# Layer 0 softmax sums in 32-column blocks beside the heads' sums, reciprocals spread by transfers, in a fused graph-attention and multi-head-attention kernel

## Chip, cores and metric

The kernel runs on one core of one Trainium2 chip. The metric is the device time of one execution in microseconds, the median over several runs. Before the change it is 2849.53 us (three runs, 2846.7 to 2849.74).

## What is computed

The input x has 64 groups of 256 tokens of width 512, and adj is a 256 x 256 mask of edges, the same for all groups. Two layers follow each other; everything is in 32-bit floats.

```python
# layer 0: graph attention, added to x
h = maximum(layernorm(x), 0)
Wh = h @ W
logits = (Wh @ a_src)[:, :, None] + (Wh @ a_dst)[:, None, :]
logits = where(logits >= 0, logits, 0.2 * logits)      # then -inf where adj == 0
x = x + softmax(logits, axis=-1) @ Wh

# layer 1: attention with 8 heads of width 64, added to x
h = maximum(layernorm(x), 0)
q, k, v = heads(h @ Wq.T + bq), heads(h @ Wk.T + bk), heads(h @ Wv.T + bv)
scores = q @ k^T / 8                                   # then -inf where adj == 0
x = x + merge(softmax(scores, axis=-1) @ v) @ Wo.T + bo
```

Both softmaxes are computed without a maximum taken off: exponentials are multiplied by a 0/1 mask, summed, and the sums' reciprocals are multiplied in. It is the sums and reciprocals of layer 0 that the change touches.

## The kernel before

One group (256 tokens, two tiles of 128 partitions) passes through a chain of stages, each a Python generator that yields between parts of its work. A hand-written list, `first_half + second_half`, is walked once for each group i; an entry such as `(aggregate0, 2)` runs the next part of that stage for group i + 2. The list is therefore the program order of every engine: each engine works through its own instructions in that order and waits by semaphores for the others. SyncE (SP) issues nearly all transfers, in the same order. PSUM has 8 banks, handed out in turn by `bank`.

The stages that matter here, with the engine that does the work:

- `weights0` (lines 518 to 561, entry E0, two groups ahead): ScalarE makes the exponentials, VectorE their maximum (L537), GpSimd applies the mask (`em`, L540) and adds the two halves of the source nodes into `esum`, 128 partitions x 256 columns (L542). In its third part TensorE multiplies `esum` by a 128 x 128 matrix of ones (L556): the product holds the softmax sum of each of the 256 target nodes in every one of 128 partitions. VectorE takes the maximum with 1e-38 (L558) and the reciprocal (L559), over 256 columns, into a tile of tag `rb0`.
- `quarters0` (L566 to 593, entry Q0, two ahead): GpSimd combines quarters of h, multiplies `em` by the reciprocals (L578) and makes four differences `eq` (L588). These are the operands of a seven-product (Strassen-like) multiplication, used for groups from PLAIN = 3 on. Groups 0 to 2 take a plain one.
- `aggregate0` (L595 to 648, entry U0, then US): seven products of h and the scaled edge weights (L606), four and then three, with sums on VectorE; ScalarE copies the first.
- `normalize0` and `normalize1` (entries N0 and N1): statistics on ScalarE, closed by three short GpSimd operations (L474 to L476), then the normalization on ScalarE; `transpose1` (X1) transposes the result of normalize1 on TensorE (L750).
- `attention` (L825 to 924, entries A and A_OLD): scores (L838), exponentials, masks (L851) and sums over the two halves (L853); then `values` (L863) and `head_sums` (L873). There eight matmuls put the sums of the 8 heads into one bank: the stationary operand `half` is 32 columns wide, so pair e of heads fills partitions 32e to 32e + 31. VectorE takes the reciprocal (L886), and eight transfers (L909), issued by SyncE, spread one row each, 256 columns, over 64 partitions of the tile `rb`. `scale` (entry AS) multiplies `aT` by it on VectorE (L936), and `output` (entry O) uses `aT` in products with Wo (L207).

For a group g, `head_sums` runs in the iteration g + 1, at the A_OLD with which the second half begins. The third E0 of that iteration, at the end of the first half, belongs to group g + 3.

Of the kernel before, what the change touches and what calls it, by code (L numbers as in the profile page):

```python
# [9 lines left out]
F32 = mybir.dt.float32  # L10
# [6 lines left out]
P = 128  # L17
# [6 lines left out]
Q = 32  # L24
# [4 lines left out]
def kernel(  # L29
# [26 lines left out]
    nc = tc.nc  # L56
    B, N, D = x.shape
    NC = N // P
    DC = D // P
    NT = GB * NC  # L60
    TOK = NT * P
    G = B // GB
    DH = D // HEADS
# [18 lines left out]
    ones = const.tile([P, P], F32, tag="ones", name="ones")  # L82
# [49 lines left out]
    def bounded():  # L132
        weights = ctx_b.enter_context(tc.tile_pool(name="weights", bufs=1))
        big = ctx_b.enter_context(tc.tile_pool(name="big", bufs=1))
        work = ctx_b.enter_context(tc.tile_pool(name="work", bufs=1))
# [3 lines left out]
        def bank(shape, name):  # L139
            return ps_mm.tile(shape, F32, tag="mm", name=name)  # L140
# [207 lines left out]
        pick = weights.tile([P, P], F32, tag="pick", name="pick")  # L348
# [10 lines left out]
        def constants():  # L359

            ok = weights.tile([P, 2 * DC + 5], F32, tag="ok", name="ok")
            rows = weights.tile([P, 2 * DC], F32, tag="rows", name="rows")
            gms = []
            for n in range(2):
                w_q = whole((wq_sb, wk_sb)[n])  # L370

                gm = work.tile([P, DC, DH], F32, tag="gram", name=f"gram_{n}", bufs=2)
                gms.append(gm)
                for pair in range(2):
                    pg = bank([P, 2, DH], f"pgram_{n}_{pair}")
                    for e in range(2):
                        for c in range(DC):
                            for r in range(2):
                                at = e * P + r * DH
                                wc = w_q[c // 2][pair][:, c % 2, at : at + DH]  # L380
                                nc.tensor.matmul(
                                    pg[r * DH : (r + 1) * DH, e, :], wc, wc,
                                    start=(c == 0), stop=(c == DC - 1),
                                )
                    yield
                    nc.vector.tensor_copy(gm[:, 2 * pair : 2 * pair + 2, :], pg)
                    yield
            for n, gm in enumerate(gms):
                pgs = [bank([P, DC, DH], f"pgram2_{n}_{r}") for r in range(2)]
                for e in range(DC):  # L390
                    for r in range(2):
                        half_p = slice(r * DH, (r + 1) * DH)
                        part = gm[half_p, e, :]
                        nc.tensor.matmul(pgs[r][half_p, e, :], part, part, start=True, stop=True)
                yield
                for e in range(DC):
                    for r in range(2):
                        half_p = slice(r * DH, (r + 1) * DH)
                        ab = work.tile([P, DH], F32, tag="gabs", name=f"gabs_{n}_{e}_{r}")
                        nc.scalar.activation(  # L400
                            ab[half_p], pgs[r][half_p, e, :], AF.Abs,
                            accum_out=rows[half_p, n * DC + e : n * DC + e + 1],
                        )
                yield
            for _ in range(10):
                yield
            sq = weights.tile([P, 4], F32, tag="sq", name="sq")
            for j, col in enumerate((cols["bq"], cols["bk"])):
                junk = work.tile([P, DC], F32, tag="e2", name=f"junk_c_{j}")
                nc.vector.scalar_tensor_tensor(  # L410
                    junk, col, 1.0, col, op0=ALU.mult, op1=ALU.mult, accum_out=sq[:, j : j + 1]
                )
            for _ in range(4):
                yield
            pq = bank([P, 2], "pq")
            nc.tensor.matmul(pq, ones, sq[:, 0:2], start=True, stop=True)
            yield
            nc.vector.tensor_scalar(
                ok[:, 2 * DC + 2 : 2 * DC + 4], pq, 1.0, None, op0=ALU.is_le
            )  # L420
            yield
            for j in range(2):
                junk = work.tile([P, D], F32, tag="e2", name=f"junk_w_{j}")
                nc.vector.scalar_tensor_tensor(
                    junk, wa[j], 1.0, wa[j], op0=ALU.mult, op1=ALU.mult, accum_out=sq[:, 2 + j : 3 + j]
                )
                yield
            nc.vector.tensor_scalar(ok[:, 0 : 2 * DC], rows, 1.0, None, op0=ALU.is_le)
            nc.vector.tensor_scalar(ok[:, 2 * DC : 2 * DC + 2], sq[:, 2:4], 1.95, None, op0=ALU.is_le)
            yield  # L430
            big_v = weights.tile([P, 1], F32, tag="big_v", name="big_v")
            nc.vector.tensor_reduce(big_v, svs, AX.X, ALU.add)
            nc.vector.tensor_scalar(
                ok[:, 2 * DC + 4 : 2 * DC + 5], big_v, 1.0e6, None, op0=ALU.is_le
            )
            okm = weights.tile([P, 1], F32, tag="okm", name="okm")
            nc.vector.tensor_reduce(okm, ok, AX.X, ALU.min)
            for _ in range(12):
                yield
            pk = bank([1, 1], "pok")  # L440
            nc.tensor.matmul(pk, okm, ones[:, 0:1], start=True, stop=True)
            nc.vector.tensor_scalar(flag, pk, P - 0.5, None, op0=ALU.is_lt)
            yield
            picks()
            yield

        class Stats:

# [30 lines left out]
        nodes, edges, sums0, lefts, norms, qkv, vs, outs = {}, {}, {}, {}, {}, {}, {}, {}  # L479
# [38 lines left out]
        def weights0(g):  # L518
# [22 lines left out]
            esum = work.tile([P, N], F32, tag="esum", name=f"esum_{g}")  # L541
            engine.tensor_tensor(esum, em[:, 0, :], em[:, 1, :], op=ALU.add)  # L542
            edges[g] = [em]
            yield

            if g == 0:
                ps = bank([P, NT], f"ps_{g}")
                for t in range(NT):
                    nc.tensor.matmul(
                        ps[:, t : t + 1], esum[:, t * P : (t + 1) * P], ones[:, 0:1],  # L550
                        start=True, stop=True,
# [7 lines left out]
            nc.vector.reciprocal(rs, rs)  # L559
            edges[g].append(rs)  # L560
            yield


        PLAIN = 3

        def quarters0(g):  # L566

# [257 lines left out]
        def attention(g):  # L825
# [30 lines left out]
            def values(j, pair):  # L856
# [13 lines left out]
                aT.append(work.tile([P, 2, N], F32, tag=f"aT{j}", name=f"aT{j}_{g}"))  # L870
                nc.scalar.copy(aT[j], pav)  # L871

            def head_sums():  # L873

                psm = bank([P, N], f"psm_{g}")
                for r in range(2):
                    for e in range(DC):
                        nc.tensor.matmul(
                            psm[e * Q : (e + 1) * Q, :],
                            half[:, r, :],  # L880
                            sums[e][:, r, :],
                            start=(r == 0),
                            stop=(r == 1),
                        )
                rc = work.tile([P, N], F32, tag="rc", name=f"rc_{g}")
                nc.vector.reciprocal(rc, psm)  # L886
                return rc

            exs = [scores(e) for e in range(DC)]
# [4 lines left out]
            if g == G - 1:  # L894
# [3 lines left out]
                rc = head_sums()  # L898
                values(1, exs[2:4])
            else:  # L900
                for j in range(2):
                    values(j, exs[2 * j : 2 * j + 2])
                rc = head_sums()
            if g < G - 2:
                rb = work.tile([P, DC, N], F32, tag="rb", name=f"rb_{g}")
                for e in range(DC):
                    for r in range(2):
                        src = rc[e * Q + r * (Q // 2) : e * Q + r * (Q // 2) + 1, :]
                        nc.sync.dma_start(  # L909
                            rb[r * DH : (r + 1) * DH, e, :],  # L910
                            bass.AP(
                                tensor=src.tensor, offset=src.offset,
                                ap=[src.ap[0], [0, DH], [1, N]],
                            ),
                        )
            else:

                yield
                rb = [bank([P, N], f"prb_{g}_{e}") for e in range(DC)]
                for e in range(DC):  # L920
                    rows = slice(e * Q, (e + 1) * Q)
                    nc.tensor.matmul(rb[e], pick[rows, :], rc[rows, :], start=True, stop=True)
            outs[g] = aT, rb
            yield

# [89 lines left out]
        def aside(n=1):  # L1015
            for _ in range(n):
                next(side, END)

        K, V, W, O = (project_qk, 0), (project_v, 0), (transform0, 1), (output, -2)
        N0, D0, E0, U0 = (normalize0, 3), (normalize0, 2), (weights0, 2), (aggregate0, 2)  # L1020
        Q0 = (quarters0, 2)
        US, N1, X1 = (aggregate0, 1), (normalize1, 1), (transpose1, 1)
        A, A_OLD, BO = (attention, 0), (attention, -1), (bias_rows, 0)
        AS, AS_OLD = (scale, -1), (scale, -2)
        first_half = [
            (load, 3), O, D0, K, AS_OLD, O, K, O, K, E0, O, K, E0, O, US, A_OLD, K, O, K, BO, O, K, E0,
        ]
        second_half = [
            A_OLD, A, Q0, A, W, N0, W, W, V, N0, W, W, W, N1, W, N1, A, V, V, V, A, N0, N1, U0, V, AS,
            U0, X1, V, X1, V, X1,  # L1030
        ]

# [259 lines left out]
```

## Time and profile before

| what | us |
|---|---|
| median of three runs | 2849.53 |
| profiled execution, whole | 2846.97 |
| its span | 2845.2 |
| TensorE busy / VectorE busy / GpSimd busy / ScalarE busy | 2828.9 / 2473.5 / 1607.0 / 1257.3 |
| L556, layer 0 sums, TensorE, 126 trace instructions | 37.8 busy |
| L558 and L559, their maximum and reciprocal, VectorE, 63 each | 25.9 and 110.4 busy |
| L878, heads' sums, TensorE, 1024 trace instructions | 68.9 busy |
| L886, their reciprocal, VectorE, 64 | 112.4 busy, 103.4 idle before |
| L909, spreading transfers of 64 KB, 496 | 4.9 from issue to landing (median) |

Busy time is the union of an engine's instructions; TensorE's are pipelined, so the duration of one matmul in the trace (382 ns for L556) is longer than the time for which it keeps the next one from starting. A 32-bit matmul of the program is two instructions in the trace. "Idle before" is the time in which the engine stood still ahead of such an instruction. One group takes 43.7 us in the middle of the run (the L556 rows at 1405.37 and 1449.11 us of the timeline), and the groups repeat each other closely.

### The profile page before, as it was taken

The numbers are of one execution on the slowest core, as the hardware profiler recorded it, in microseconds if no ns is written. First come the engines' busy times: TensorE is split into PE (matmuls) and PEld (weight loads), VectorE is DVE, ScalarE is ACT, GpSimd is POOL, SyncE is SP. The second block draws the span as 40 slices with busy tenths as digits, with TensorE's granted clock in tenths as the row PEclk, the third lists the DMA queues.
The fourth block names the chain that finished last, engine by engine and source line by source line (L and its number), as shares of the span: only waits on it lengthen the run. The fifth ranks groups of instructions, "written<-read, shape, count | busy, mean of one in ns | idle before, by whom it ended". The sixth has DMA issues, their size and how long they took to land. (4 is left out here: it accounts for less than half of the span.)

```text
span 2845.2 us, 53317 instructions
## 1 busy us (share of the span) xinstructions
PE 2828.9 (99%) x20316; PEld 2472.3 (87%) x20316; DVE 2473.5 (87%) x3946; ACT 1257.3 (44%) x3045; POOL 1607.0 (56%) x2016
## 2 busy tenths in 40 slices
PE   9999999999999999999999999999999999999998
PEld 6888988988889889888898898888988988889886
DVE  7998988888889888888898888888988888889875
ACT  5444444443444444434444444344454443444532
POOL 2656556566565565665655655656556556565541
PEclk9999999999999999999999999999999999999999
DMA  4122122221221222212212222122122221221221
GB/s 134 23 38 38 34 42 33 36 45 31 38 38 34 42 33 36 45 31 38 39 33 42 33 36 46 31 38 40 32 42 33 36 45 31 38 42 30 34 42 27
DMA packets 82826, 111.01 MB, mean 39 GB/s; under 512 B 11524, under 2 KB 48644, under 8 KB 82566
## 3 DMA queue, kind: packets, MB, share of 16 engines
q1 hardware_dynamic: 82470, 107.53, 23.7%
q8 instruction: 164, 2.69, 0.4%
q14 instruction: 96, 0.79, 0.1%
q0 software_dynamic: 96, 0.01, 0.0%
HBM read 41.43 MB, written 33.55 MB: 26 GB/s over the span
## 5 line engine op out<-in xcount | busy, mean ns | idle before, releaser
L701 DVE TENSOR_TENSOR x<-po,x 128x1024 f32<-128x1024 f32 x875 | 593.8, 685 | 130.2 <-PE po L207 122.9
L851 DVE TENSOR_TENSOR ex<-ex,maskT 128x512 f32<-128x512 f32 x512 | 435.3, 890 | 0.0
L474 POOL TENSOR_SCALAR ve<-ssq 128x2 f32<-128x2 f32 x127 | 25.1, 198 | 483.8 <-ACT h L463 250.6
L846 ACT ACTIVATE ex<-psc 128x512 f32<-128x512 f32 x512 | 257.7, 627 | 89.5 <-PE psc L838 89.4
L871 ACT COPY aT<-pav 128x512 f32<-128x512 f32 x128 | 74.9, 585 | 499.2 <-PE pav L863 468.1
L511 DVE SCALAR_TENSOR_TENSOR junk<-wa,h 128x512 f32<-128x512 f32 x252 | 276.6, 1098 | 7.9 <-ACT h L504 1.1
L216 PEld LDWEIGHTS pqk<-hs,wq_sb 128*128 128x128 f32 x2016 | 264.4, 192 | 12.9
L216 PE MATMUL pqk<-hs,wk_sb 128*128 128x128 f32 x2016 | 266.3, 275 | 0.0
L216 PE MATMUL pqk<-hs,wq_sb 128*128 128x128 f32 x2016 | 265.8, 275 | 0.0
L207 PE MATMUL pv<-wv_sb,hs 128*128 128x256 f32 x1024 | 262.9, 380 | 0.6 <-DVE v L194 0.5
L540 POOL TENSOR_TENSOR em<-e,maskT 128x512 f32<-128x512 f32 x62 | 79.6, 1283 | 321.7 <-DVE e L537 312.0
L207 PE MATMUL po<-wo_sb,as 128*128 128x256 f32 x992 | 255.2, 380 | 0.0
L207 PE MATMUL po<-w_sb,us 128*128 128x256 f32 x1008 | 248.5, 379 | 0.0
L216 PEld LDWEIGHTS pqk<-hs,wk_sb 128*128 128x128 f32 x2016 | 245.4, 192 | 0.0
L838 PE MATMUL psc<-qk 64*128 64x256 f32 x2048 | 239.0, 383 | 0.3 <-DVE rc L886 0.3
L863 PE MATMUL pav<-ex,v 128*64 128x256 f32 x2048 | 235.4, 382 | 0.0
L838 PEld LDWEIGHTS psc<-qk 64*128 64x128 f32 x2048 | 193.1, 187 | 46.9 <-issue 25.0
L165 POOL TENSOR_TENSOR hs<-hT 128x256 f32<-128x256 f32 x64 | 47.0, 735 | 319.2 <-PE pv L207 319.2
L853 DVE TENSOR_TENSOR sm<-ex 128x512 f32<-128x512 f32 x256 | 210.5, 822 | 8.9
L863 PEld LDWEIGHTS pav<-ex,v 128*64 128x64 f32 x2048 | 141.2, 137 | 85.8 <-issue 20.3
L207 PEld LDWEIGHTS po<-w_sb,us 128*128 128x128 f32 x1008 | 191.4, 190 | 26.3 <-DVE x L701 0.3
L216 PEld LDWEIGHTS pqk<-hT,wq_sb 128*128 128x128 f32 x1512 | 198.2, 192 | 9.6
(211 smaller groups left out, 6564.5 us busy)
## 6 DMA issues: line engine op xcount, KB each, us to landing
x<-in_x_dram SPq DMA_DIRECT2D x64, 512.0 KB, 5.6
out_dram<-x SPq DMA_DIRECT2D x128, 256.0 KB, 2.0
rb<-rc SPq DMA_DIRECT2D x496, 64.0 KB, 4.9
wq_sb<-in_L_gnn_Wq_dram SPq DMA_DIRECT2D x4, 256.0 KB, 8.4
wk_sb<-in_L_gnn_Wk_dram SPq DMA_DIRECT2D x4, 256.0 KB, 6.7
w_sb<-in_L_gnn_W_dram SPq DMA_DIRECT2D x4, 256.0 KB, 6.6
wv_sb<-in_L_gnn_Wv_dram SPq DMA_DIRECT2D x4, 256.0 KB, 6.6
wo_sb<-in_L_gnn_Wo_dram SPq DMA_DIRECT2D x4, 256.0 KB, 6.0
```

The costliest lines, as they stand in the source:

```text
L165: nc.gpsimd.tensor_tensor(s[:, 0], a(1, 0), a(1, 1), op=ALU.add)
L207: nc.tensor.matmul(dst[:, 0:HD], left[:, c, :], wt[:, slot, c, :], start=c == 0, stop=c == 1)
L216: nc.tensor.matmul(dst[:, at : at + P], wt[:, slot, c, e * P : (e + 1) * P], left[:, c, :], start=c == 0, stop=c == 1,)
L511: nc.vector.scalar_tensor_tensor(junk, (wa if g else pas)[a], 1.0, h[:, t, :], op0=ALU.mult, op1=ALU.mult, accum_out=dst[:, t : t + 1],)
L540: engine.tensor_tensor(em, e1, maskT, op=ALU.mult)
L701: nc.vector.tensor_add(dst, src, dst)
L838: nc.tensor.matmul(psc[r][:, m, :], qk[rows, 2 + e % 2, m * P : (m + 1) * P], qk[rows, e % 2, :], start=True, stop=True,)
L846: nc.scalar.activation(ex[:, r, :, :], psc[r], AF.Exp, scale=SCALE)
L851: nc.vector.tensor_mul(ex[:, r, :, :], ex[:, r, :, :], maskT)
L853: nc.vector.tensor_add(sm, ex[:, :, 0, :], ex[:, :, 1, :])
L863: nc.tensor.matmul(pav[r * DH : (r + 1) * DH, i, :], v[j][:, m, at : at + DH], pair[i][:, r, m, :], start=(m == 0), stop=(m == NC - 1),)
L871: nc.scalar.copy(aT[j], pav)
```

## The change

For groups from 3 on, `weights0` ends after its second part: it keeps `esum`, and its product with the ones, the maximum and the reciprocal over 256 columns are gone. In their place `head_sums` of group g also makes the layer 0 sums of group g + 3, where there is one. Its bank is 64 columns wider. Four matmuls, each with 32 columns of ones as the stationary operand and a quarter of `esum` (64 columns) as the moving one, put quarter e of the 256 sums into partitions 32e to 32e + 31 of these 64 columns, ahead of the heads' own eight. VectorE takes maximum and reciprocal over the 64 columns, and then the heads' reciprocal. Four transfers on SyncE's queue, ahead of the eight for the heads, spread one row of 64 columns each over all 128 partitions of a tile of tag `rb0`, which `quarters0` reads as before. In the program order the third E0 leaves the first half, and one V (a value product) moves ahead of the first U0. A scratch tile of the set-up shares the buffer of the reciprocals, and `PLAIN` is defined earlier.

```diff
@@ -396,7 +396,7 @@
                 for e in range(DC):
                     for r in range(2):
                         half_p = slice(r * DH, (r + 1) * DH)
-                        ab = work.tile([P, DH], F32, tag="gabs", name=f"gabs_{n}_{e}_{r}")
+                        ab = work.tile([P, DH], F32, tag="rc", name=f"gabs_{n}_{e}_{r}")
                         nc.scalar.activation(
                             ab[half_p], pgs[r][half_p, e, :], AF.Abs,
                             accum_out=rows[half_p, n * DC + e : n * DC + e + 1],
@@ -444,6 +444,9 @@
             picks()
             yield
 
+
+        PLAIN = 3
+
         class Stats:
 
 
@@ -541,7 +544,12 @@
             esum = work.tile([P, N], F32, tag="esum", name=f"esum_{g}")
             engine.tensor_tensor(esum, em[:, 0, :], em[:, 1, :], op=ALU.add)
             edges[g] = [em]
-            yield
+            if g >= PLAIN:
+
+                edges[g].append(esum)
+            yield
+            if g >= PLAIN:
+                return
 
             if g == 0:
                 ps = bank([P, NT], f"ps_{g}")
@@ -559,9 +567,6 @@
             nc.vector.reciprocal(rs, rs)
             edges[g].append(rs)
             yield
-
-
-        PLAIN = 3
 
         def quarters0(g):
 
@@ -870,20 +875,48 @@
                 aT.append(work.tile([P, 2, N], F32, tag=f"aT{j}", name=f"aT{j}_{g}"))
                 nc.scalar.copy(aT[j], pav)
 
+            def spread(dst, row):
+
+                nc.sync.dma_start(
+                    dst,
+                    bass.AP(
+                        tensor=row.tensor, offset=row.offset,
+                        ap=[row.ap[0], [0, dst.shape[0]], [1, dst.shape[1]]],
+                    ),
+                )
+
             def head_sums():
 
-                psm = bank([P, N], f"psm_{g}")
+                psm = bank([P, N + DH], f"psm_{g}")
+                rc = work.tile([P, N + DH], F32, tag="rc", name=f"rc_{g}")
+                g0 = g + PLAIN
+                if g0 < G:
+
+                    part = slice(N, N + DH)
+                    for e in range(DC):
+                        rows = slice(e * Q, (e + 1) * Q)
+                        nc.tensor.matmul(
+                            psm[rows, part], ones[:, 0:Q], edges[g0][1][:, e * DH : (e + 1) * DH],
+                            start=True, stop=True,
+                        )
                 for r in range(2):
                     for e in range(DC):
                         nc.tensor.matmul(
-                            psm[e * Q : (e + 1) * Q, :],
+                            psm[e * Q : (e + 1) * Q, 0:N],
                             half[:, r, :],
                             sums[e][:, r, :],
                             start=(r == 0),
                             stop=(r == 1),
                         )
-                rc = work.tile([P, N], F32, tag="rc", name=f"rc_{g}")
-                nc.vector.reciprocal(rc, psm)
+                if g0 < G:
+
+                    nc.vector.tensor_scalar_max(rc[:, part], psm[:, part], 1e-38)
+                    nc.vector.reciprocal(rc[:, part], rc[:, part])
+                    rb0 = work.tile([P, N], F32, tag="rb0", name=f"rb0_{g0}")
+                    for e in range(DC):
+                        spread(rb0[:, e * DH : (e + 1) * DH], rc[e * Q : e * Q + 1, part])
+                    edges[g0][1] = rb0
+                nc.vector.reciprocal(rc[:, 0:N], psm[:, 0:N])
                 return rc
 
             exs = [scores(e) for e in range(DC)]
@@ -905,21 +938,15 @@
                 rb = work.tile([P, DC, N], F32, tag="rb", name=f"rb_{g}")
                 for e in range(DC):
                     for r in range(2):
-                        src = rc[e * Q + r * (Q // 2) : e * Q + r * (Q // 2) + 1, :]
-                        nc.sync.dma_start(
-                            rb[r * DH : (r + 1) * DH, e, :],
-                            bass.AP(
-                                tensor=src.tensor, offset=src.offset,
-                                ap=[src.ap[0], [0, DH], [1, N]],
-                            ),
-                        )
+                        at = e * Q + r * (Q // 2)
+                        spread(rb[r * DH : (r + 1) * DH, e, :], rc[at : at + 1, 0:N])
             else:
 
                 yield
                 rb = [bank([P, N], f"prb_{g}_{e}") for e in range(DC)]
                 for e in range(DC):
                     rows = slice(e * Q, (e + 1) * Q)
-                    nc.tensor.matmul(rb[e], pick[rows, :], rc[rows, :], start=True, stop=True)
+                    nc.tensor.matmul(rb[e], pick[rows, :], rc[rows, 0:N], start=True, stop=True)
             outs[g] = aT, rb
             yield
 
@@ -1023,10 +1050,10 @@
         A, A_OLD, BO = (attention, 0), (attention, -1), (bias_rows, 0)
         AS, AS_OLD = (scale, -1), (scale, -2)
         first_half = [
-            (load, 3), O, D0, K, AS_OLD, O, K, O, K, E0, O, K, E0, O, US, A_OLD, K, O, K, BO, O, K, E0,
+            (load, 3), O, D0, K, AS_OLD, O, K, O, K, E0, O, K, E0, O, US, A_OLD, K, O, K, BO, O, K,
         ]
         second_half = [
-            A_OLD, A, Q0, A, W, N0, W, W, V, N0, W, W, W, N1, W, N1, A, V, V, V, A, N0, N1, U0, V, AS,
+            A_OLD, A, Q0, A, W, N0, W, W, V, N0, W, W, W, N1, W, N1, A, V, V, V, A, N0, N1, V, U0, AS,
             U0, X1, V, X1, V, X1,
         ]
 
```

## The prediction

> **What bounds the kernel now.** I read the page's busy shares first, then the waits, then the timeline of one steady group for each engine (the 44 us from 1399 to 1443), and last the rows of the operations that the change touches.
>
> ```profile
> span 2845.2 us, 53317 instructions
> PE 2828.9 (99%) x20316; PEld 2472.3 (87%) x20316; DVE 2473.5 (87%) x3946; ACT 1257.3 (44%) x3045; POOL 1607.0 (56%) x2016
> DVE rc L886 <- PE psm L878: 103.4, 63, 3.9
> ACT xn L729 <- POOL nmr L476: 17.0, 62, 1.6
> ```
>
> TensorE is busy for 2828.9 of 2845.2 us, and its clock row is full in every slice. No TensorE wait stands among the large ones: the other engines wait for it. So only two things count: how long TensorE's own list of instructions is, and whether the change makes it wait.
>
> ```profile
> 34.78 2.09 PE L381 MATMUL pgram<-wk_sb 128*64 128x64 f32 x64
> 36.80 1.99 PE L770 MATMUL pqk<-hT,wq_sb 128*128 128x256 f32 x8
> ...
> 1405.37 0.60 PE L556 MATMUL ps<-esum,ones 128*128 128x256 f32 x2
> 1405.89 3.67 PE L863 MATMUL pav<-ex,v 128*64 128x256 f32 x32
> 1409.50 1.07 PE L878 MATMUL psm<-sm,half 128*32 128x256 f32 x16
> 1410.50 3.73 PE L838 MATMUL psc<-qk 64*128 64x256 f32 x32
> ...
> 1427.74 0.60 PE L750 MATMUL pt<-ident,xn 128*128 128x128 f32 x4
> ...
> 1430.35 1.03 PE L207 MATMUL po<-wo_sb,aT 128*128 128x256 f32 x4
> 1431.21 1.05 PE L216 MATMUL pqk<-hT,wq_sb 128*128 128x128 f32 x8
> ```
>
> Differences of starts in this timeline are TensorE's real cost. A program matmul is two trace instructions. The layer 0 sum (L556) holds the engine from 1405.37 to 1405.89, 0.52 us. A full-width 256-column pass costs 0.215 us (four of po in 0.86 us), so two are 0.43 us, and 0.09 us is the change to the narrower tiles of pav. The heads' sums (L878) put 16 passes into 1.00 us: they run four abreast, one per 32-column block, four rounds of 0.216 us and another 0.1 us of change. The 64-column products of L381 run two abreast: 64 in 2.02 us, about 30 ns each after the change of shape.
>
> ```profile
> 1411.28 1.41 POOL L578 TENSOR_TENSOR em<-em,rb 128x256 f32<-128x256 f32 x2
> 1412.65 0.90 POOL L588 TENSOR_TENSOR eq<-em 128x128 f32<-128x128 f32 x1
> ...
> 1415.24 0.46 POOL L588 TENSOR_TENSOR eq<-em,eq 128x128 f32<-128x128 f32 x1
> 1419.78 0.19 POOL L474 TENSOR_SCALAR ve<-ssq 128x2 f32<-128x2 f32 x1 [4.09 <-ACT h L463]
> ...
> 1424.08 0.19 POOL L474 TENSOR_SCALAR ve<-ssq 128x2 f32<-128x2 f32 x1 [3.04 <-ACT xn L463]
> 1412.42 6.97 SPq L909 DMA_DIRECT2D rb<-rc  x8
> DMA to landing us min/median/max: 4.5/5.2/6.0
> ```
>
> GpSimd scales the edge weights at 1411.28, forms their differences until 1415.70, then idles 4.09 us. SyncE needs 6.97 us to issue the eight broadcasts of the heads' reciprocals, each landing about 5 us after its issue.
>
> **What the Trainium skill says.** "TensorEngine Tiling (Array Packing)", Key Properties: changing the tiling mode drains TensorE, and tiles load weights and multiply in parallel. The trace agrees: 0.09 us at the changes, four passes abreast in psm. "DMA: Bandwidth & Descriptors", Why small descriptors are slow (HBM only): a 256-byte descriptor takes 256/32 + 3 = 11 cycles, and on-chip transfers do not suffer otherwise; but its Specifications say that below 512 B a transfer is read-modify-write. No transfer of data in 256-byte pieces is in this trace, so that is the open price. "SBUF — State Buffer", Who interferes with whom: a VectorE operation with two SBUF inputs contends with GpSimd reading SBUF. The trace agrees: the two mask products at 1421.70, GpSimd idle, take 1.28 us; those at 1443.17, beside GpSimd, 2.51 us.
>
> **The change, part by part.** It acts for g0 = 3 to 63, 61 groups.
>
> TensorE loses L556: 0.43 us a group. The change of tiling stays, since the previous product now goes straight to pav. It gains four matmuls of 64 columns, eight passes, ahead of psm and in psm's own tiling, so no change is added. Cheapest: four abreast, two rounds of 60 ns (the pace of a pair of L381), 0.12 us. Dearest: no better than L381's two abreast, 8 x 30 ns = 0.25 us. I take 0.13, as psm shows four abreast. Net 0.30 us a group (0.18 to 0.31), or 61 x 0.30 = 18.3 us (11 to 19).
>
> VectorE loses the maximum and the reciprocal over 256 columns: 0.44 + 1.75 us. It gains both over 64 columns. Their rows give 0.159 and 0.166 us at 2 columns, 0.411 and 1.753 us at 256, so in between I estimate 0.22 and 0.55 us. It is 1.4 us lighter a group and worth nothing by itself: VectorE waits for TensorE here (103.4 us before the heads' reciprocal, 1.6 us in each group).
>
> The new chain, on the clock of the group shown. Pav starts at 1405.46, the new sums at about 1409.07 and end by 1409.35; VectorE starts 0.07 us later, as it does after psm now, and has the small reciprocal at about 1410.25. The heads' reciprocal behind it waits for psm until 1410.3, so it loses nothing.
>
> SyncE then issues four transfers of 32 KB (128 pieces of 256 B), ahead of the eight. An issue of the eight takes 0.47 to 1.45 us, the first four of this group 2.43 us together; I take 2.5 us. Landing of the fourth after the first issue: lower end 1.9 + 4.4 = 6.3 us (three issues and the least landing); upper end, if a piece costs as much as one of 1 KB and the four thus weigh as eight of the present, 6.0 + 4.9 = 10.9 us. By the skill's 11 cycles against 35 for 1 KB they weigh 128 x 11 / (64 x 35) = 0.63 of the present ones; I take 6.5 us, so 1416.8.
>
> Behind the waiting scaling on GpSimd stand the differences, then the statistics of the next layer 0 (the first L474) and of layer 1 (the second). From 1416.8, scaling and differences (4.4 us) end at 1421.2, the first statistics (1.3 us) at 1422.5; the second are not due before 1424.08 - 0.30 = 1423.8. That leaves 1.3 us. The aggregation that reads the differences comes after 1424.3 now (one value product is put before it), later than it needs. If the second statistics are late, ScalarE's normalization, its copy of the aggregate, VectorE's sums and the heads' scaling are late in turn, and then TensorE's products at 1427.74 and 1430.35. The swap in the order helps there: the two value sums fill the 0.57 us that VectorE now idles for that copy, so I estimate the scaling done 1.1 us ahead of its product. TensorE waits only if the fourth transfer lands later than 1419.2, about 9 us after the first issue; contention of GpSimd's moved work with the mask products near 1421.4 can cut this to 8.
>
> The eight transfers start 0.35 us later (1412.8) and queue behind the four: last landing at about 1416.8 + 8 x 0.9 = 1424.0, 0.9 us being their pace (6.4 us from first to last landing over seven). Their scaling starts near 1428.3, so 4 us remain. The load of x behind them slips by 3 us and is needed in the next group. Nothing of either is paid. Renaming the buffer of the set-up's absolute values and the side work's few moved steps touch only the first groups: nothing.
>
> **Sum.** The profiled execution took 2846.97 us (span 2845.2 and 1.8 around it): 2846.97 - 18.3 = 2828.7. The median of the runs shown lies 2.56 us above it, so I predict 2849.53 - 18.3 = 2831.2, rounded to 2831.
>
> **Rivals.**
> Late transfers, slower: the four are bound by pieces, land 10.9 us after the first issue and so 2 us beyond the point where TensorE begins to wait. Then 2831 + 61 x 2.0 = 2953. For it: the read-modify-write sentence, and transfers that already crowd (the longest issue of the eight here takes 1.39 us). Against it: half the bytes, all 128 partitions as targets, 2.5 us to spare. Break-even lies 0.3 us past the point where waiting begins. Chance 0.14.
> Short passes not abreast: each of the eight holds the engine 54 ns (a quarter of 0.215 us), 0.43 in all, and what was removed comes back: 2849. For it: weights are loaded for each pass. Against it: psm loads four abreast as well. Chance 0.07.
> Partly paid: a wait of 0.10 to 0.20 us a group through the contention named above, 6 to 12 us given back: 2837 to 2843, taken as 2840. For it: ScalarE already waits 0.27 us a group for the second statistics. Chance 0.11.
> That the change does not do what it says I exclude: in the order of the built program the full-width sum is gone from these 61 groups.
>
> **How the numbers follow.** My forecast, 2828 to 2838, has 0.68. About 0.2% (5.7 us) is what a measurement of this kernel tells from no change. Faster: 0.68 and nearly all of the partly paid case, 0.78; within 0.2%: 0.08; slower: 0.14. The range must leave out the late transfers; the low end takes the whole L556 slot as gained with nothing added (61 x 0.43 = 26, 2823) cut to 2826 as unlikely, the high end the partly paid case and a little beyond, 2844.
>
> **What would show it.** Right: the 256-column sum left for groups 1 and 2 alone; a row of eight short passes between pav and psm, 0.1 to 0.15 us from start to start; groups 43.45 instead of 43.75 us apart; GpSimd's scaling waiting for a DMA by 4 to 6 us a group, with no TensorE wait from it. Wrong: TensorE idle before pt, before the aggregation or before the output product with aT; the transfers of rb0 landing more than 8 us after the first issue; short passes further apart than 0.05 us.

## The result, and the profile after

The changed kernel takes 2828.78 us (median of 4 runs, 2827.07 to 2829.28) against 2849.55 us before (2846.7 to 2849.74): a ratio of 0.9928, 95% interval 0.9911 to 0.9946. The profiled execution took 2829.04 us, its span is 2827.2 us, 18.0 us less than before.

The page of the changed kernel (span, then busy time and share of each engine), and from its waits who waited for whom (total us, times, longest):

```profile
span 2827.2 us, 54416 instructions
PE 2810.5 (99%) x20682; PEld 2466.5 (87%) x20682; DVE 2342.2 (83%) x3946; ACT 1259.0 (45%) x3045; POOL 1579.9 (56%) x2016
...
POOL em L583 <- DMA rb<-rc: 361.9, 60, 6.8
DVE rc L913 <- PE psm L904: 203.0, 60, 3.5
```

TensorE is still busy for 99% of the span: its busy time fell by 18.4 us, as the span fell by 18.0. VectorE is busy for 131 us less; it waits longer instead, for psm 203.0 us where it was 103.4. GpSimd has a new wait of 6 us a group for the transfers, and no large TensorE wait follows from it: the largest is 4.9 us over the whole run, as before.

The timeline of TensorE in a steady group of the changed kernel (start, length, operation):

```profile
1397.49 3.67 PE L868 MATMUL pav<-ex,v 128*64 128x256 f32 x32
1401.10 0.32 PE L898 MATMUL psm<-esum,ones 128*32 128x64 f32 x8
1401.23 1.05 PE L904 MATMUL psm<-sm,half 128*32 128x256 f32 x16
1402.21 3.72 PE L843 MATMUL psc<-qk 64*128 64x256 f32 x32
...
1419.45 0.60 PE L755 MATMUL pt<-ident,xn 128*128 128x128 f32 x4
...
1422.06 1.03 PE L207 MATMUL po<-wo_sb,aT 128*128 128x256 f32 x4
...
1440.91 0.65 PE L868 MATMUL pav<-ex,v 128*64 128x256 f32 x4
```

The full-width sum is gone, the eight short passes hold TensorE from 1401.10 to 1401.23, 0.13 us, and the next group's pav starts 43.42 us after this one's. Before, the sums of two groups stood 43.74 us apart. The difference of 0.32 us, 61 times, is 19.5 us.

The other engines of the same group. The rows are SyncE's issues, then GpSimd's scaling, its last difference and the two statistics, then ScalarE's copy of the aggregate, then VectorE's maximum and the heads' scaling:

```profile
1403.22 10.38 SPq L880 DMA_DIRECT2D rb<-rc  x12
1409.44 1.41 POOL L583 TENSOR_TENSOR em<-em,rb 128x256 f32<-128x256 f32 x2 [6.09 <-DMA rb<-rc]
...
1412.18 0.46 POOL L593 TENSOR_TENSOR eq<-em,eq 128x128 f32<-128x128 f32 x1
1412.72 0.19 POOL L477 TENSOR_SCALAR ve<-ssq 128x2 f32<-128x2 f32 x1
...
1415.79 0.19 POOL L477 TENSOR_SCALAR ve<-ssq 128x2 f32<-128x2 f32 x1 [1.64 <-ACT xn L466]
...
1418.73 0.35 ACT L622 COPY uT<-pu 128x256 f32<-128x256 f32 x1
1402.35 0.23 DVE L913 TENSOR_SCALAR rc<-psm 128x64 f32<-128x64 f32 x1 [3.38 <-PE psm L904]
...
1420.34 1.29 DVE L963 TENSOR_TENSOR aT<-aT,rb 128x512 f32<-128x512 f32 x2
```

The scaling begins 6.2 us after the first issue. Scaling and differences take 3.2 us here, not 4.4 as before; at this later place VectorE adds products out of PSUM beside the differences, where before it multiplied masks. Two slacks can be read off: GpSimd idles 1.64 us before the second statistics, and the copy of the aggregate ends at 1419.08, 0.37 us before the transposes (pt) start.

### The profile page after: what moved, and what is told of

It reads as the page before. It is cut to its first block, busy times and chain, and to the rows that moved or that the text cites. A ratio compares the mean times of both kernels' runs of the same rounds, so it can differ in the third digit from the quotient of the medians.

```text
span 2827.2 us, 54416 instructions
## 1 busy us (share of the span) xinstructions
PE 2810.5 (99%) x20682; PEld 2466.5 (87%) x20682; DVE 2342.2 (83%) x3946; ACT 1259.0 (45%) x3045; POOL 1579.9 (56%) x2016
## 5 line engine op out<-in xcount | busy, mean ns | idle before, releaser
L856 DVE TENSOR_TENSOR ex<-ex,maskT 128x512 f32<-128x512 f32 x512 | 402.0, 826 | 0.0
L583 POOL TENSOR_TENSOR em<-em,rb 128x256 f32<-128x256 f32 x122 | 86.8, 733 | 361.9 <-DMA rb<-rc 361.9
L207 PE MATMUL pv<-wv_sb,hs 128*128 128x256 f32 x1024 | 252.7, 379 | 0.6 <-DVE v L194 0.5
L207 PEld LDWEIGHTS po<-w_sb,us 128*128 128x128 f32 x1008 | 191.4, 190 | 26.3 <-DVE x L706 0.3
L207 PEld LDWEIGHTS pv<-wv_sb,hs 128*128 128x128 f32 x1024 | 189.5, 190 | 24.5 <-DVE v L194 0.9
L858 DVE TENSOR_TENSOR sm<-ex 128x512 f32<-128x512 f32 x256 | 202.4, 791 | 8.9
```

Of the source, the lines that this page charges most:

```text
L207: nc.tensor.matmul(dst[:, 0:HD], left[:, c, :], wt[:, slot, c, :], start=c == 0, stop=c == 1)
L583: nc.gpsimd.tensor_tensor(em[:, m, :], em[:, m, :], rb, op=ALU.mult)
L856: nc.vector.tensor_mul(ex[:, r, :, :], ex[:, r, :, :], maskT)
L858: nc.vector.tensor_add(sm, ex[:, :, 0, :], ex[:, :, 1, :])
```

## Experiments

The runs were made in several series. In them the kernel before took between 2847.16 and 2849.55 us (medians), so a difference from the changed kernel's 2828.78 us, measured in another series, is good to about 2 us. "So many us a group" is a difference divided by the 61 groups on which the change acts.

### One part at a time: TensorE's slot, VectorE's load, the order

Two kernels start from the one before. One leaves out only the product:

```diff
-                ps = bank([P, N], f"ps_{g}")
-                nc.tensor.matmul(ps, ones, esum, start=True, stop=True)
+                ps = esum
+                if g < PLAIN:
+                    ps = bank([P, N], f"ps_{g}")
+                    nc.tensor.matmul(ps, ones, esum, start=True, stop=True)
```

> The kernel before with the full-width layer 0 product (L556) left out for the groups from 3 on; the maximum and the reciprocal over 256 columns stay on VectorE and read esum itself, so the softmax sums of layer 0 are left out of the result. Theory: TensorE's list of instructions sets the time, and the slot is worth 0.43 us a group: 61 x 0.43 = 26 us less than before, about 2823. Rival (VectorE's load sets the time, since it loses 1.4 us a group in the change): VectorE's list is as long as before, so no change, about 2849.

The other leaves out only the maximum and the reciprocal:

```diff
-                rs = work.tile([P, N], F32, tag="rb0", name=f"rb0_{g}")
-            nc.vector.tensor_scalar_max(rs, ps, 1e-38)
-            nc.vector.reciprocal(rs, rs)
+                rs = work.tile([P, N], F32, tag="rb0", name=f"rb0_{g}") if g < PLAIN else None
+            if g >= PLAIN:
+                rs = maskT[:, 0, :]
+            else:
+                nc.vector.tensor_scalar_max(rs, ps, 1e-38)
+                nc.vector.reciprocal(rs, rs)
```

> The kernel before with the product L556 kept and the maximum and reciprocal (L558, L559) left out for the groups from 3 on; GpSimd multiplies by a row of the mask instead of the reciprocals, so layer 0's division is left out. VectorE loses 2.2 us a group, more than in the change. Theory: VectorE waits for TensorE here, so nothing is gained: 2849, within 4 us. Rival (VectorE's load): at least the whole gain of the change, 2829 or less.

Without the product: 2821.21 us against 2847.47 us before in these runs, ratio 0.991 (0.9894 to 0.9927), 26.3 us less. Without the vector work: 2846.86 us, ratio 0.9998 (0.999 to 1.0007). Its page shows what happened to the freed time, in its busy shares and one of its waits:

```profile
PE 2830.5 (99%) x20316; PEld 2473.6 (87%) x20316; DVE 2347.4 (82%) x3824; ACT 1258.7 (44%) x3045; POOL 1608.3 (56%) x2016
...
DVE rc L889 <- PE psm L881: 231.0, 64, 3.9
```

VectorE is 126 us less busy, and its wait for psm grew from 103.4 to 231.0 us: all of it went into waiting.

Two kernels start from the changed one. One gives VectorE its work back:

```diff
             if g >= PLAIN:
+                back = work.tile([P, N], F32, tag="gram", name=f"back_{g}", bufs=2)
+                nc.vector.tensor_scalar_max(back, esum, 1e-38)
+                nc.vector.reciprocal(back, back)
+                yield
                 return
...
-            ... O, K, BO, O, K,
+            ... O, K, BO, O, K, E0,
```

> The changed kernel with the third E0 put back and in it a maximum and a reciprocal over 256 columns of esum into a scratch tile that nobody reads: VectorE gets back what it lost, and keeps the short ones. Theory: no change against the changed kernel, 2827 to 2832. Rival (VectorE's load): back to the time before, about 2849.

The other undoes the swap in the list:

```diff
-            ... A, N0, N1, V, U0, AS,
+            ... A, N0, N1, U0, V, AS,
```

> The changed kernel with the value product put back behind the first aggregation step, as before. Theory: the swap only widens the room ahead of the heads' scaling (VectorE idles again for about 0.5 us for ScalarE's copy, and the scaling ends about 0.4 us ahead of its product instead of 1 us): 2827 to 2833. Rival (the swap carries part of the gain, or the later edge weights need it): 5 to 20 us slower than the changed kernel, 2834 to 2849.

With the vector work back (VectorE is busy for 2474.4 us again): 2829.43 us (2828.4 to 2830.27). In the old order: 2828.47 us (2827.07 to 2831.16). Neither differs from the changed kernel's 2828.78. VectorE's relief and the swap are worth nothing here; the slot on TensorE is the gain. The swap's use as a reserve was not tried together with late transfers.

### The price of the short passes

```diff
-                    for e in range(DC):
+                    for e in [*range(DC)] * 3:
                         rows = slice(e * Q, (e + 1) * Q)
                         nc.tensor.matmul(
                             psm[rows, part], ones[:, 0:Q], edges[g0][1][:, e * DH : (e + 1) * DH],
```

> The changed kernel with the four short matmuls of the layer 0 sums done three times over, same operands and same place. Theory: they run four abreast at about 0.065 us a round, so 16 more passes are 4 rounds, 0.26 us a group, 61 x 0.26 = 16 us: 2845 (2842 to 2848). Rival 1 (the short passes are hidden in the change of tiling or the weight loads): 2829. Rival 2 (not abreast, 0.054 us each): 61 x 0.86 = 53 us, 2881.

Measured: 2840.89 us (2840.07 to 2841.95), 12.1 us more than the changed kernel. TensorE's timeline of this kernel:

```profile
1405.99 0.54 PE L898 MATMUL psm<-esum,ones 128*32 128x64 f32 x24
1406.35 1.05 PE L904 MATMUL psm<-sm,half 128*32 128x256 f32 x16
```

24 passes take 0.36 us where eight took 0.13, so 16 more cost 0.23 us: 58 ns for a round of four. 61 times that is 14 us, a little over the 12.1 seen and below the 16 expected; the time lies 1 us under the expected range. The passes are neither free nor one after another.

### How much later may the transfers be?

The forecast rests on the four transfers being hidden. Four kernels put extra transfers of the same kind ahead of them (one, two, three, four); a fifth puts eight, with a second scratch tile. The edit shown is that with four; the kernel with eight has `range(2)` in its first line:

```diff
+                    for d in range(1):
+                        spare = work.tile([P, N], F32, tag="gram", name=f"spare{d}_{g0}", bufs=2)
+                        for e in range(DC):
+                            spread(spare[:, e * DH : (e + 1) * DH], rc[e * Q : e * Q + 1, part])
                     for e in range(DC):
                         spread(rb0[:, e * DH : (e + 1) * DH], rc[e * Q : e * Q + 1, part])
```

> The changed kernel with four more transfers of the same kind (32 KB, one row to 128 partitions, into a scratch tile) issued ahead of the four. Theory: the fourth needed transfer lands 2.0 to 2.7 us later, about 8.6 us after the first issue instead of 6.2, still just before TensorE begins to wait (8.9): 2829 to 2835. Rival (the transfers are already at the edge, every microsecond of delay is paid): 61 x 2.3 = 140 us more, 2970.

> The same with eight more transfers ahead. Theory: the fourth needed one lands about 11 us after the first issue, some 2 us beyond the point where TensorE begins to wait, and the heads' eight land too late for their scaling as well: about 61 x 2 = 122 us more, 2950 (2900 to 3010), with TensorE waiting before the transposes of layer 1 or the output product. Rival (GpSimd's scaling has far more room than reckoned): below 2840.

A sixth issues the four behind the heads' eight:

```diff
-                    for e in range(DC):
-                        spread(rb0[:, e * DH : (e + 1) * DH], rc[e * Q : e * Q + 1, part])
...
                         spread(rb[r * DH : (r + 1) * DH, e, :], rc[at : at + 1, 0:N])
+                if g + PLAIN < G:
+                    for e in range(DC):
+                        spread(
+                            edges[g + PLAIN][1][:, e * DH : (e + 1) * DH],
+                            rc[e * Q : e * Q + 1, N : N + DH],
+                        )
```

> The changed kernel with the four transfers issued behind the heads' eight instead of ahead of them. Theory: the first of the twelve can only go once the heads' reciprocal is done (1.6 us later), eight issues take 7 us and four 2.5, so the fourth lands about 14.8 us after the point at which it is issued first now, 5 to 6 us beyond the point where TensorE begins to wait: 61 x 5.5 = 335 us more, about 3160 (3050 to 3250). Rival (the order of the queue doesn't matter, the transfers share 16 engines anyway): below 2840.

Four more: 3126.4 us (3117.64 to 3127.83), not 2829 to 2835. Eight more, run once: 3222.43 us, not 2900 to 3010. Behind the heads, run once: 3253.37 us, just above the 3050 to 3250 expected. The delay is paid at a higher rate than reckoned, and it begins sooner. The kernel with four more, GpSimd and TensorE:

```profile
1414.83 1.42 POOL L583 TENSOR_TENSOR em<-em,rb 128x256 f32<-128x256 f32 x2 [9.07 <-DMA rb<-rc]
1416.20 0.91 POOL L593 TENSOR_TENSOR eq<-em 128x128 f32<-128x128 f32 x1
...
1424.97 1.12 PE L755 MATMUL pt<-ident,xn 128*128 128x128 f32 x4 [2.99 <-ACT uT L622]
1425.88 1.92 PE L207 MATMUL pv<-wv_sb,hT 128*128 128x256 f32 x4
1427.58 0.72 PE L755 MATMUL pt<-ident,xn 128*128 128x128 f32 x4
```

The first issue of its group is at 1405.55, so the scaling starts 9.3 us after it, 3.1 us later than in the changed kernel; the differences are slow again (0.91 us for the first one against 0.47), and TensorE idles 2.99 us. Then its passes are slow as well: the value product takes 1.70 us to the next start instead of 0.86. From this run the room was reckoned anew and three more kernels were made, with one, two and three extra transfers. They have one scratch tile, and in place of `range(DC)` in its loop `range(1)`, `range(2)` and `range(3)`.

> The changed kernel with one extra 32 KB transfer ahead of the four. After the run with four extra ones (298 us slower) the theory of the room is corrected: GpSimd's second statistics give 1.6 us, and TensorE's transpose is released by ScalarE's copy of the aggregate, 0.4 us ahead of it, so the room is 2.0 us of delay as long as GpSimd's differences stay clear of VectorE's mask products. One extra delays the landing by 0.6 to 0.9 us: nothing paid, 2829 (2826 to 2833). First reckoning (2.5 us and more): the same. Rival (any delay is paid): 61 x 0.8 = 49 us more, 2878.

> Two extra transfers ahead of the four. Corrected theory: the landing moves by about 1.7 us, the differences end within the mask products and take a little longer, so the 2.0 us are just used up: 2829 to 2845. First reckoning (room of 2.5 us): 2829. Rival (any delay is paid): 61 x 1.7 = 104 us more, 2933.

> Three extra transfers ahead of the four. Corrected theory: the landing moves by about 2.4 us, the differences and the first statistics take some 1 us longer beside the mask products, so TensorE waits about 1.4 us a group, and if its clock is lowered after such a wait as with four extra ones, up to 1.5 us more: 61 x (1.4 to 2.9) = 85 to 177 us more, 2914 to 3006. First reckoning (room of 2.5 us, no contention): 2829 to 2835.

| extra transfers | GpSimd's wait a group, us | median, us | against the changed kernel, us |
|---|---|---|---|
| 0 | 6.0 | 2828.78 | |
| 1 | 7.3 | 2861.99 | +33 |
| 2 | 8.7 | 3081.04 | +252 |
| 3 | 8.7 | 3077.47 | +249 |
| 4 | 9.1 | 3126.4 | +298 |
| 8 | 12.4 | 3222.43 (one run) | +394 |

The wait is the row `POOL em L583 <- DMA` of each kernel's waits over its count. One extra already costs 33 us (ratio to before 1.0046, interval 1.0029 to 1.0063), which neither reckoning expected; two and three miss their ranges too (2829 to 2845 and 2914 to 3006). The rows of the kernel with one extra say why:

```profile
1429.71 1.42 POOL L583 TENSOR_TENSOR em<-em,rb 128x256 f32<-128x256 f32 x2 [7.30 <-DMA rb<-rc]
...
1432.46 0.99 POOL L593 TENSOR_TENSOR eq<-em,eq 128x128 f32<-128x128 f32 x1
1433.53 0.52 POOL L477 TENSOR_SCALAR ve<-ssq 128x2 f32<-128x2 f32 x1
1434.13 1.15 POOL L478 TENSOR_TENSOR rstd<-ve,minus_half 128x2 f32<-128x2 f32 x1
...
1435.64 0.19 POOL L477 TENSOR_SCALAR ve<-ssq 128x2 f32<-128x2 f32 x1
...
1432.46 1.54 DVE L856 TENSOR_TENSOR ex<-ex,maskT 128x512 f32<-128x512 f32 x2
...
1437.37 1.52 ACT L734 ACTIVATE xn<-x,nmr,rstd 128x512 f32<-128x512 f32 x2 [0.26 <-POOL nmr L479]
1438.80 0.35 ACT L622 COPY uT<-pu 128x256 f32<-128x256 f32 x1
1439.20 0.66 PE L755 MATMUL pt<-ident,xn 128*128 128x128 f32 x4 [0.55 <-ACT uT L622]
```

Pav starts at 1416.53 there. The scaling comes 13.18 us after it, in the changed kernel 11.95: 1.23 us late. The last difference takes 0.99 us instead of 0.46, and the first statistics last until 1435.56, 2.03 us instead of 1.43. VectorE's mask products (1432.46 to 1434.00) and the sum behind them (to 1434.72) now lie beside them. The transfers are not what slows GpSimd: the three differences just before took 0.46 us each, with the 16 DMA engines as busy (0.85 of the time, against 0.94 beside the slow one). So 1.23 us of delay has become 2.4 us at the end of the first statistics; 1.6 us of it are absorbed. The second statistics are slowed too (a further 0.2 us), the copy is 1.0 us late, and about 0.3 us is absorbed ahead of the transposes. They start 0.7 us later after pav than in the changed kernel; 0.55 us of it shows as TensorE's idle time. By the medians the loss is 33 us over 61 groups, 0.54 us. The room is thus 0.5 to 0.7 us of delay, because moving the work makes it slower.

The jump from one extra to two, 3.6 us a group, has two parts of about the same size. One is the wait itself, which grows from 0.55 to 2.33 us: the scaling starts 9.0 us after the first issue, not 7.5. The other is the clock. The windows of the kernels with one and with two extra, around and after the wait (stretch; its length; busy of TensorE, weight load, VectorE, ScalarE, GpSimd; TensorE clock; DMA share and GB/s):

```profile
1438.50:1439.25 0.75, 0.20 (x3) 0.05 (x1) 0.11 (x2) 0.65 (x2) 0.00 (x0) 1.00 0.15 57
1439.25:1442.50 3.25, 3.25 (x19) 2.93 (x20) 3.12 (x8) 1.08 (x2) 0.33 (x1) 1.00 0.00 0
```

```profile
1406.46 1.00 PE L755 MATMUL pt<-ident,xn 128*128 128x128 f32 x4 [2.33 <-ACT uT L622]
...
1404.00:1406.50 2.50, 0.17 (x3) 0.05 (x1) 0.50 (x3) 1.83 (x4) 0.52 (x2) 1.00 0.53 199
1406.50:1409.70 3.20, 3.20 (x12) 2.73 (x13) 3.07 (x8) 0.50 (x1) 0.00 (x0) 0.52 0.00 0
```

After a wait of 0.55 us TensorE goes on at full clock. After one of 2.33 us it is granted 0.52 on average over the next 3.2 us. Windows of half a microsecond put the clock at 0.50 from 1406.6 to 1410.0, 3.4 us, so 1.7 us are lost. The whole run agrees: its mean granted clock is 0.967 against 0.999 in the changed kernel, 1.6 us a group. Wait and clock make 4.0 us in this group; 252 us over 61 groups are 4.1.

### A shorter TensorE list elsewhere

If TensorE's list sets the time, the sixteen passes of psm (0.98 us a group) are worth shortening. The summands of the heads' sums and the matrix `half` become 16-bit bf16; the summands are rounded, the sums still add up in 32 bits.

```diff
-    half = const.tile([P, 2, Q], F32, tag="half", name="half")
+    half = const.tile([P, 2, Q], mybir.dt.bfloat16, tag="half", name="half")
...
-                sm = work.tile([P, 2, N], F32, tag="sm", name=f"sm_{g}_{e}", bufs=4)
+                sm = work.tile([P, 2, N], mybir.dt.bfloat16, tag="sm", name=f"sm_{g}_{e}", bufs=4)
```

> The changed kernel with the summands of the heads' sums (sm) and the matrix half in 16-bit bf16 instead of 32-bit floats: the summands are rounded to 8 bits of mantissa, the sums still add up in 32 bits. The heads' eight matmuls should then be eight trace instructions instead of sixteen. Theory (TensorE's list sets the time): psm shrinks from four rounds of 0.216 us to two, or to less if a 16-bit pass is shorter too: 0.43 to 0.65 us a group, 64 groups, 28 to 42 us less than the changed kernel, 2787 to 2801. Rival (VectorE, whose list stays, or the chain behind psm sets the time): 2829.

Measured: 2788.54 us (2787.92 to 2788.98), ratio to before 0.9792 (0.9775 to 0.9808), 40.2 us less than the changed kernel. TensorE's timeline:

```profile
1425.76 0.32 PE L898 MATMUL psm<-esum,ones 128*32 128x64 f32 x8
1425.90 0.40 PE L904 MATMUL psm<-sm,half 128*32 128x256 bf16 x8
1426.23 3.72 PE L843 MATMUL psc<-qk 64*128 64x256 f32 x32
```

From start to start psm takes 0.33 us instead of 0.98: 0.65 us a group, 64 groups, 42 us. It is the fastest of all kernels here, at the price of 16-bit rounding of those summands.

## Why the prediction was right, and where its reserve was not

**The gain.** "Net 0.30 us a group, 18.3 us" held: 0.13 us for the short passes as taken, 0.32 us a group between starts, 18.0 us in the span and 20.8 us in the medians, whose runs scatter by about 3 us. That the slot alone is the gain is shown by leaving out each part alone: 26.3 us for the product (0.43 times 61 was 26), nothing for the vector work.

**VectorE's work.** The two short operations were put at 0.22 and 0.55 us and took 0.23 and 0.55 us. But the step from the end of the new sums to the maximum, "VectorE starts 0.07 us later", failed. In the changed kernel the maximum waits for the heads' passes too (its releaser is L904, which writes the same bank) and starts at 1402.35, 4.86 us after pav instead of 3.96: 0.9 us late. The first issue moved with it.

**The transfers.** The landing was reckoned at 6.5 us after the first issue; GpSimd starts 6.2 us after it. The bound from piece size (10.9 us) was not reached: the small transfers land in a median of 3.8 us against 5.0 for the heads'. That this came out near is no proof of the weight 0.63, an estimate from the Trainium skill's 11 cycles: the page, "DMA: Bandwidth & Descriptors" (Why small descriptors are slow (HBM only)), gives them as part of a penalty that it says transfers within SBUF don't have, and no run here separates the price of a piece from the fixed part of a landing. Whatever the read-modify-write below 512 B that the same page names (Specifications) costs, it did not reach the size feared.

**The heads' transfers and the order.** Twelve issues take 10.38 us. The last transfer lands at about 1417.9, and the heads' scaling at 1420.34 did not wait; 2.4 us remain where 4 were reckoned. The first of its two operations, 0.69 us long, ends about 1.0 us ahead of the product at 1422.06, near the 1.1 estimated for the swap; but without the swap the time is the same.

**The step that failed: the room.** "TensorE waits only if the fourth transfer lands later than 1419.2, about 9 us after the first issue; contention can cut this to 8." The runs put that point at 6.7 to 6.9 us, 0.5 to 0.7 us past the real landing; the "2.5 us to spare" of the prediction were not there. Four of its terms were off:

- The first issue came 0.9 us later after pav, which took 0.9 us of the room.
- Behind the second statistics 1.1 us more were reckoned. The transposes are released by ScalarE's copy of the aggregate, and that left 0.37 us: 0.7 us less.
- GpSimd's work, once it reaches the mask products, needs 1.3 us more (0.53 in the difference, 0.60 and 0.2 in the statistics). The prediction named this contention and allowed 1 us for it.
- Scaling, differences and first statistics take 4.7 us, where 5.7 were reckoned: 1.0 us more room.

Together they turn 8.9 us into 7.0, close to what was found. The last term was not foreseen and was luck: by these numbers, an estimate, the room would have ended ahead of the real landing without it. The forecast stood because the landing was right and this term helped, not because the reserve was as wide as stated. The late-transfer rival was too cheap by the same token: it had 2 us a group and no lowered clock, while four extra transfers, with the scaling 9.3 us after the first issue, cost 4.9 us a group.

## What to carry to other kernels

When one engine is busy all the time, measure in starts, not durations, what an edit takes out of its list, and give relief to other engines no value. Before work is hidden behind a transfer, find the room by delaying that transfer on purpose: moved work may run beside other operations and slow down, so a slack read off the old timeline is too wide. A wait of the bounding engine can cost more than its length once it is long enough to lower its clock.

## What the runs showed of the hardware

- In the groups looked at, TensorE's granted clock fell to 0.50 for 3.4 us with waits of 2.33, 2.39 and 2.99 us (two, three and four extra transfers); the fall came 2.4 to 3.2 us after the wait began, in one case 0.8 us after TensorE had gone on. It stayed at 1.00 after waits of 0.55 us (one extra) and 1.69 us (eight extra). The Trainium skill's page "TensorE: Matmul & The Clock Gate" (Why this matters for your kernels) warns of idle gaps over about 3 us; here 2.33 us were enough.
- Four column-blocked 32-bit passes abreast take 58 ns a round at 64 columns; 16-bit passes of 256 columns need 0.33 us for eight, with the change of tiling in it.
- A 128 x 128 difference on GpSimd took 0.46 us beside VectorE's additions out of PSUM and 0.99 us beside its mask products.
- Extra transfers delay the following ones unevenly: in a group of each trace the scaling starts 6.2, 7.5, 9.0, 9.0, 9.3 and 13.1 us after the first issue with none, one, two, three, four and eight. Why two weigh as much as three was not settled.
